# Two inner sums of the third head's products, issued directly behind the second head's last running sum

## The chip, the cores and the metric

The kernel runs on one core of a Trainium2 chip. The core has a matrix engine (TensorE, PE in the profile; its weight loads are listed as PEld), a vector engine (VectorE, DVE), an activation engine (ScalarE, ACT), GpSimd (POOL) and a sync engine (SP). Each works through a queue of its own in order. The metric is the device time of one execution in microseconds (us); several executions are timed and their median is taken. A profile is one execution recorded instruction by instruction.

## The reference

Sixteen images x of 512 channels by 32 x 32 positions (1024 positions) in float32:

```
xn  = group_norm(x, 8 groups)
q, k, v = qkv_w @ xn + qkv_b            # 1536 x 512 by 512 x 1024, per image
attn = softmax(q^T k / sqrt(128))       # 4 heads of 128 channels, 1024 x 1024 each
out = proj_w @ (attn v) + proj_b        # 512 x 512 by 512 x 1024
return x + out
```

## The kernel before, in words

**The loop.** The main loop runs over steps: 16 images, 4 heads of each (numbered 0 to 3), 8 key blocks j of each head. In a step, for each half of the 1024 queries, `scores` (L798) multiplies a block of k by q into PSUM, ACT takes the exponential (L804), and DVE adds the block of exponentials to a running sum `tot` (L810 for the first pair of blocks, L812 from j = 2 on). The instruction of each L812 is kept in `added[image, head, j]`. `weighted_sum` (L894) multiplies the exponentials of the step before by v into the PSUM tile `po`; behind a head's last block ACT copies `po` out (L901). A head that is over gets its denominators from `tot` (a transpose on L821, a reduction on L823, small operations from L826 to L835) and a division (L904).

**The products between.** All other matrix products are cut into units that are spread over the steps by `plan_head`. Head 0 of an image carries the q and k products of its own heads 2 and 3, head 1 the output projection of the image before, head 2 the q and k products for heads 0 and 1 of the next image, and head 3 the v product of the next image. So behind head 1's last step the projection of one image ends, and the q/k product of another begins.

**How such a product is computed.** `two_levels` uses Strassen's scheme in Winograd's form twice: seven outer products in four groups (`OUTER`: products 1 and 5, 2 and 6, 7 and 4, 3), and for each group seven inner products in the order 1, 2, 6, 5, 7, 4, 3 (`ORDER`). An inner product is two matrix products here, one for each outer product of the group, and each shows up as two PE instructions of 128 x 256 (L567). Inner products 1, 6, 7 and 4 gather in one PSUM bank (`x` in the profile's names, as `qk_x`), 2 alone and then 5 and 3 in another (`qk_y`). Between, ACT copies the `x` bank away (L461, `qk_p`, `qk_u`), and DVE adds the `y` bank to such a copy (L587, `qk_r`). Each inner product multiplies a weight factor by a block or by a sum of blocks (`FACTORS`): products 1, 2 and 3 use the blocks b11, b21 and b22 as they are, and

```
t1 = b12 - b11   (for product 5)       t2 = b22 - t1   (for product 6)
t3 = t2 - b11    (for product 7)       t4 = b21 - t2   (for product 4)
```

`make_sum` (L529 to L541) takes one such inner sum of a group: a `tensor_sub` on DVE of 128 x 256 for each of the group's outer products (L537), and where `sums == "keep"` a copy of it to DRAM, issued on POOL's queue (L541), which the v product reads later. `sums` is "keep" for the q/k products of heads 0 and 1 of every image but image 0, and these are the products that head 2 carries. For their group 0 (outer products 1 and 5) the first outer product reads the image's own tiles x, and the second reads an outer sum that lies in x too (L283 `x<-x`). Their first unit holds the group's weights, the sums t1 and t2 and inner product 1; the second unit t3 and product 2; the third t4 and product 6; the fourth product 5; the fifth product 7.

**The projection's end.** `finish` in `proj_groups` (L775) adds to each quarter of the result its bias and residual (L778) and a last part (L781), and sends it out with a DMA on POOL's queue (L782).

**What sets the order.** A scheduler lays down each engine's queue before the run. It goes by priority, which is the order of the program, among the instructions that its own model of time takes for ready; `tc.high_priority(URGENT)` moves what stands in its block 40 places forward in this priority, and `tc.issue_after(ins)` puts what stands in its block behind `ins` in the queue of that engine, which is an order and not a wait for a result. On the chip each queue is then worked off in that order.

Of the kernel before, what the change touches and what calls it, by code (L numbers as in the profile page):

```python
# [27 lines left out]
URGENT = 40  # L28
# [135 lines left out]
def fast_path(ctx, tc, x, sources, out, consts, flag, dims):  # L164
# [6 lines left out]
    nc = tc.nc  # L171
    B, C, N, NCC, NH2, NB, GC, SCALE = dims
# [324 lines left out]
    def two_levels(name, site, b, blocks, finish, sums="make", homes="BBBB", prepare=None):  # L497
# [13 lines left out]
        def sum_tile(g, m):  # L511
            k = int(m[1]) - 1
            tag = f"in_{m}" if homes[g] == "B" else f"ot{2 + k // 2}{k % 2}"
            if homes[g] == "C":
                if k % 2 == 0:
                    pairs[g] = ppool.tile([P, N], F32, tag="p", name=f"{name}_{g}_{m}")
                t = pairs[g][:, ts(k % 2, HALF)]
            else:
                t = tpool.tile([P, HALF], F32, tag=tag, name=f"{name}_{g}_{m}")
            haves[g][m] = t.rearrange("p (i q) -> p i q", q=Q)  # L520
            return haves[g][m][:, : len(OUTER[g])]

        def inner_block(g, i, m):
            if m[0] == "t":
                return haves[g][m][:, i, :]
            outer = blocks()[FACTORS[OUTER[g][i]][1]]
            return outer[int(m[1]) - 1][:, ts(int(m[2]) - 1, Q)]

        def make_sum(g, m):  # L529
            n = len(OUTER[g])  # L530
            to = sum_tile(g, m)
            a, c = {
                "t1": ("b12", "b11"), "t2": ("b22", "t1"), "t3": ("t2", "b11"),
                "t4": ("b21", "t2"),
            }[m]
            for i in range(n):
                nc.vector.tensor_sub(to[:, i, :], inner_block(g, i, a), inner_block(g, i, c))  # L537
            if sums == "keep":
                t = dpool.tile([P, n, Q], F32, tag=f"{m}_{g}", bufs=1, name=f"kept_{m}_{g}")
                inner_kept[b, g, m] = t  # L540
                nc.gpsimd.dma_start(t, to)  # L541

        def group_units(g):
# [12 lines left out]
            def inner_sum(m):  # L556
                if sums != "load" and m not in have:
                    make_sum(g, m)
# [57 lines left out]
        def first_sums(groups=(0,)):  # L616
            for g in groups:
                for m in ("t1", "t2", "t3", "t4"):
                    if sums == "load":
                        nc.sync.dma_start(sum_tile(g, m), inner_kept[b, g, m])  # L620
                    else:
                        make_sum(g, m)
# [165 lines left out]
    inverse, rows_of, added, exps = {}, {}, {}, {}  # L788
    steps = B * HEADS * NB

    def where(s):
        bh, j = divmod(s, NB)
        return (*divmod(bh, HEADS), j)
# [336 lines left out]
    for s in range(steps + 1):  # L1130
        units = []
        if s < steps:
            b, h, j = where(s)
# [9 lines left out]
        for half in range(NH2):  # L1143
# [11 lines left out]
            n = (len(units) + 1) // 2  # L1155
# [137 lines left out]
```

## Time and profile before

| what | value |
|---|---|
| median of 5 runs | 3181.52 us (3180.82 to 3183.71) |
| the profiled execution | 3181.88 us; span of its instructions 3180.0 us |
| PE busy | 3163.4 us, 99% of the span |
| DVE busy | 2630.4 us, 83% |
| ACT busy | 1440.6 us, 45% |
| POOL busy | 514.8 us, 16% |
| TensorE clock granted | 0.998 of full |

A line of the timeline gives start and length in us, engine, line of the kernel, operation, what it writes and reads, its shape, how many instructions of the kind were merged (x2), and in brackets how long the engine was idle before it and what ended that. Matrix products overlap each other, and the end of one is a model; the distance from one start to the next says how long the engine was taken.

### The profile page before, as it was taken

The page shows a single profiled execution, that of the slowest core. Times are in us where ns is not written, and L with a number is a line of the kernel's source. Part 1 is how long each engine was busy: PE and PEld are TensorE (multiplying, and loading weights), DVE is VectorE, ACT ScalarE, POOL GpSimd, SP SyncE. Part 2 cuts the span into 40 slices and gives each one's busy share as a digit, 9 for nine tenths or more (in the row PEclk, how much of TensorE's full clock was granted, in tenths as well). Part 3 has the DMA queues.
Part 4 walks back from the last instruction along what each step waited for, and adds up shares of the span by engine and source line. Part 5 has one row for each costly group of instructions (what it writes and reads, how often), then busy time and mean ns, then how long its engine had stood idle before and what let it go on. Part 6 is the DMA issues. An engine that isn't in the chain of part 4 may idle for free.

```text
span 3180.0 us, 34082 instructions
## 1 busy us (share of the span) xinstructions
PE 3163.4 (99%) x10496; PEld 2187.1 (69%) x10496; DVE 2630.4 (83%) x4634; ACT 1440.6 (45%) x2709; POOL 514.8 (16%) x893
## 2 busy tenths in 40 slices
PE   9999999999999999999999999999999999999999
PEld 7566676676766766677666677667676676766764
DVE  8878979788897888878888787987879978788784
ACT  2535435354353543535435454453534545344342
POOL 0011221111211112211122111222012221122200
PEclk9999999999999999999999999999999999999999
DMA  5655554545545555454554545555455564555631
GB/s 168 213 183 162 182 177 146 178 150 194 166 157 164 161 184 176 163 166 145 193 171 160 174 141 190 167 173 173 140 179 170 176 188 127 181 160 184 182 126 41
DMA packets 211308, 526.92 MB, mean 166 GB/s; under 512 B 32816, under 2 KB 65840, under 8 KB 211120
## 3 DMA queue, kind: packets, MB, share of 16 engines
q1 hardware_dynamic: 133312, 284.74, 29.5%
q0 software_dynamic: 63840, 204.53, 19.1%
q10 hardware_dynamic: 13968, 35.41, 3.5%
q8 instruction: 86, 1.41, 0.2%
q14 instruction: 102, 0.84, 0.1%
HBM read 389.56 MB, written 135.00 MB: 165 GB/s over the span
## 4 chain that ended last, share of the span: by engine, by line
PE 87%; DVE 10%; issue 2%; POOL 1%; DMA 1%; SPq 0%; ACT 0%; POOLq 0%; DVEq 0%
PE po L894 24%; PE s L798 24%; PE qk_x L567 12%; PE qk_y L567 9%; PE v_x L567 6%; PE v_y L567 4%; PE pp_x L567 4%; PE pp_y L567 3%; DVE y L781 2%; DVE tot L812 2%; DVE y L778 2%; DVE pp_r L587 1%; DVE pp_r L634 1%; POOL rstd L68 1%; DVE o L904 1%
## 5 line engine op out<-in xcount | busy, mean ns | idle before, releaser
L894 PE MATMUL po<-p,v 128*128 128x512 f32 x2048 | 1048.9, 594 | 0.0
L798 PE MATMUL s<-qk,qk 128*128 128x512 f32 x2048 | 1047.1, 593 | 1.3 <-ACT p L804 1.3
L804 ACT ACTIVATE p<-s 128x512 f32<-128x512 f32 x1024 | 610.3, 596 | 933.6 <-PE s L798 930.2
L894 PEld LDWEIGHTS po<-p,v 128*128 128x128 f32 x2048 | 602.9, 303 | 316.8 <-issue 212.2
L812 DVE TENSOR_TENSOR tot<-tot,p 128x1024 f32<-128x1024 f32 x385 | 469.2, 1219 | 161.6 <-ACT p L804 161.6
L798 PEld LDWEIGHTS s<-qk,qk 128*128 128x128 f32 x2048 | 387.6, 190 | 89.2 <-issue 28.0
L567 PEld LDWEIGHTS qk_x<-qk_t,w 128*128 128x128 f32 x1344 | 250.5, 190 | 171.5 <-issue 76.6
L567 PE MATMUL qk_x<-qk_t,w 128*128 128x256 f32 x1344 | 357.4, 382 | 1.1 <-ACT qk_u L461 1.1
L461 ACT COPY qk_u<-qk_x 128x512 f32<-128x512 f32 (+1 forms) x256 | 136.2, 532 | 230.6 <-PE qk_x L567 226.2
L731 POOL DMA_DIRECT2D vd<-vu x120 | 66.7, 557 | 908.6 <-DVE vu L723 901.3
L587 DVE TENSOR_TENSOR qk_r<-qk_y,qk_u 128x512 f32<-128x512 f32 (+1 forms) x256 | 157.8, 616 | 36.4 <-ACT qk_u L461 22.0
L567 PE MATMUL pp_x<-pp_t,w_proj 128*128 128x256 f32 x630 | 169.3, 385 | 0.0
L736 POOL DMA_DIRECT2D v<-vd x240 | 140.5, 592 | 170.4 <-DMA vd<-vu 74.9
L782 POOL DMA_DIRECT2D out_y<-y x120 | 66.0, 550 | 628.6 <-DVE y L781 626.5
L587 DVE TENSOR_TENSOR v_r<-v_y,v_u 128x512 f32<-128x512 f32 (+1 forms) x120 | 76.2, 635 | 110.6 <-ACT v_u L461 80.3
L567 PE MATMUL v_x<-v_t,w_v 128*128 128x256 f32 x630 | 166.6, 381 | 0.0
L541 POOL DMA_DIRECT2D kept_t<-qk_t x240 | 129.2, 540 | 223.5 <-DVE qk_t L537 204.0
L567 PEld LDWEIGHTS pp_x<-pp_t,w_proj 128*128 128x128 f32 x630 | 116.1, 190 | 64.1 <-issue 22.2
L567 PEld LDWEIGHTS v_x<-v_t,w_v 128*128 128x128 f32 x630 | 118.4, 190 | 55.3 <-issue 19.1
L567 PE MATMUL qk_y<-x,w 128*128 128x256 f32 x512 | 141.8, 379 | 0.0
L666 DVE SCALAR_TENSOR_TENSOR qk<-qk_r,qkb_sb,qk_r 128x512 f32<-128x512 f32 x192 | 137.6, 743 | 1.6
L461 ACT COPY v_u<-v_x 128x512 f32<-128x512 f32 (+1 forms) x124 | 66.2, 534 | 157.0 <-PE v_x L567 130.4
(204 smaller groups left out, 4481.3 us busy)
## 6 DMA issues: line engine op xcount, KB each, us to landing
kept_t<-qk_t POOLq DMA_DIRECT2D x180, 256.0 KB, 3.2
w<-kept SPq DMA_DIRECT2D x90, 512.0 KB, 4.2
v_t<-kept_t SPq DMA_DIRECT2D x180, 256.0 KB, 2.9
w<-kept SPq DMA_DIRECT2D x90, 384.0 KB, 3.5
rinv<-row ACTq DMA_DIRECT2D x63, 512.0 KB, 4.7
x<-in_x POOLq DMA_DIRECT2D x60, 512.0 KB, 5.0
vd<-vu POOLq DMA_DIRECT2D x120, 256.0 KB, 3.1
v<-vd POOLq DMA_DIRECT2D x240, 128.0 KB, 4.2
```

Of the source, the lines that this page charges most:

```text
L461: nc.scalar.copy(t[n][:, :width], t["x"][:, :width])
L541: nc.gpsimd.dma_start(t, to)
L567: nc.tensor.matmul(acc[:, ts(i, Q)], have["w"][t][:, i, slot, :], inner(i, bn), start=(first and i == 0), stop=True, skip_group_check=True,)
L587: nc.vector.tensor_add(dst, view(a), view(c))
L666: nc.vector.scalar_tensor_tensor(st[b, h][:, ts(half, HALF)], a, qkb_sb[:, i : i + 1], c, ALU.add, ALU.add)
L731: nc.gpsimd.dma_start(rows[which][ts(h, P), :], u)
L736: nc.gpsimd.dma_start(vs[b, pair][ts(q, BLK), half].rearrange("m h (k i) j -> m (h k) (i j)", k=n), rows[which].rearrange("(k m) (q e) -> ...
L782: nc.gpsimd.dma_start(out[b, ts(o, P), ts(half, HALF)], t)
L798: nc.tensor.matmul(sc, ks[b, h][:, ts(j, P)], qs[b, h][:, ts(half, HALF)], start=True, stop=True)
L804: exps[s] = nc.scalar.activation(ps[s][:, ts(half, HALF)], sc, AF.Exp, scale=SCALE)
L812: added[b, h, j] = nc.vector.tensor_add(tot[b, h][:, i], tot[b, h][:, i], ps[s][:, i])
L894: nc.tensor.matmul(po[b, h][:, i], v_block(b, h, j), ps[s][:, i], start=(j == 0), stop=(j == NB - 1),)
```

## The change

In `make_sum`, the subtractions of t1 and t2 of group 0 in the "keep" products stand now in two blocks: they are issued behind the last running sum of head 1 (`added[b - 1, 1, NB - 1]`; b is the image that the product belongs to, so b - 1 is the image whose heads are being worked off), and at a priority 40 places further forward. The arithmetic, the DMAs and all other instructions are as before.

```diff
-            for i in range(n):
-                nc.vector.tensor_sub(to[:, i, :], inner_block(g, i, a), inner_block(g, i, c))
+            with ExitStack() as order:
+                if sums == "keep" and g == 0 and m in ("t1", "t2"):
+
+
+                    order.enter_context(tc.issue_after(added[b - 1, 1, NB - 1].ins))
+                    order.enter_context(tc.high_priority(URGENT))
+                for i in range(n):
+                    nc.vector.tensor_sub(
+                        to[:, i, :], inner_block(g, i, a), inner_block(g, i, c)
+                    )
```

## The prediction

> **What bounds the kernel now.** First the page: its busy times, and the chain of work that ended last.
>
> ```profile
> PE 3163.4 (99%) x10496; PEld 2187.1 (69%) x10496; DVE 2630.4 (83%) x4634; ACT 1440.6 (45%) x2709; POOL 514.8 (16%) x893
> ...
> PE 87%; DVE 10%; issue 2%; POOL 1%; DMA 1%; SPq 0%; ACT 0%; POOLq 0%; DVEq 0%
> ```
>
> PE sets the time, and 10% of the chain runs through DVE: PE can gain only where it waits. So I read the chain itself in order of time, around the place the change touches: the start of the third head (head 2), here the fourth of fourteen such places. A line gives start, length, work.
>
> ```profile
> 932.46 1.13 DVE tot L812
> 933.60 0.60 DVE y L781
> 934.20 0.66 DVE y L778
> ...
> 935.80 0.35 DVE qk_t L537
> 936.15 0.04 issue
> 936.19 0.70 PE qk_y L567 x2
> ```
>
> From 910 us on, the chain lies on DVE. It comes back to PE at 936.19, through a subtraction on L537, the second half of t1. The timeline of PE and then of DVE shows the place whole:
>
> ```profile
> 934.58 1.02 PE L894 MATMUL po<-p,v 128*128 128x512 f32 x2
> 935.44 0.59 PE L567 MATMUL qk_y<-qk_t,w 128*128 128x256 f32 x2
> 936.19 0.70 PE L567 MATMUL qk_y<-qk_t,w 128*128 128x256 f32 x2 [0.16 <-DVE qk_t L537]
> 936.73 1.02 PE L798 MATMUL s<-qk,qk 128*128 128x512 f32 x2
> 937.58 1.03 PE L567 MATMUL qk_x<-qk_t,w 128*128 128x256 f32 x4
> 938.45 1.04 PE L894 MATMUL po<-p,v 128*128 128x512 f32 x2
> 939.32 1.10 PE L567 MATMUL qk_x<-qk_t,w 128*128 128x256 f32 x4
> 940.25 0.59 PE L567 MATMUL qk_x<-x,w 128*128 128x256 f32 x2
> ```
>
> ```profile
> 932.39 1.21 DVE L812 TENSOR_TENSOR tot<-tot,p 128x1024 f32<-128x1024 f32 x1
> 933.52 0.68 DVE L781 TENSOR_TENSOR y<-y,pp_r 128x512 f32<-128x512 f32 x1
> 934.12 0.74 DVE L778 SCALAR_TENSOR_TENSOR y<-pp_r,projb_sb,y 128x512 f32<-128x512 f32 x1
> 934.78 0.41 DVE L537 TENSOR_TENSOR qk_t<-x 128x256 f32<-128x256 f32 x1
> 935.12 0.68 DVE L781 TENSOR_TENSOR y<-y,pp_r 128x512 f32<-128x512 f32 x1
> 935.72 0.41 DVE L537 TENSOR_TENSOR qk_t<-x 128x256 f32<-128x256 f32 x1
> 936.06 0.68 DVE L587 TENSOR_TENSOR qk_r<-qk_y,qk_p 128x512 f32<-128x512 f32 x1
> 936.66 0.74 DVE L537 TENSOR_TENSOR qk_t<-x,qk_t 128x256 f32<-128x256 f32 x2
> 937.33 0.75 DVE L537 TENSOR_TENSOR qk_t<-qk_t,x 128x256 f32<-128x256 f32 x2
> ```
>
> DVE is never idle here (8.00 us busy between 930 and 938). Behind the last running sum (932.39) come two of the projection's last additions, the first half of t1 (934.78), an addition, the second half of t1 (935.72), the eviction L587, t2, t3. On PE, 935.44 is inner product 5, which needs t1: its second half starts 0.06 us behind the end of 935.72. Product 6 (937.58) needs t2; product 7 (939.32) needs t3 and ACT's copy of what 6 left in the bank.
>
> **What that wait costs.** The bracket says 0.16 us, measured from a modelled end; starts are better. Scores take 0.85 us (936.73 to 937.58), four instructions of 128 x 256 take 0.87 (937.58 to 938.45). From 935.44 to 937.58 PE does 0.87 + 0.85 = 1.72 us of work in 2.14: **0.42 us are lost**, 0.32 ahead of 936.19 and 0.10 inside that pair. A second loss follows: product 7 takes 0.93 us (939.32 to 940.25) for 0.87 of work, having waited for the copy of 6 (its weight load at 939.28 is put down to ACT qk_u), so 0.06.
>
> The place recurs in the timeline once an image, 196.2 us apart, behind each projection: in images 1 to 14, that is 14 times (image 0 has no projection before, image 15 no next image), as the waits on L537 count (PE qk_y, 14 times). Twelve lose 0.42. Two, at 739 and 2309 us, lose 0.56: 739.04 to 741.28 is 2.24 against 1.72, with 0.04 more ahead of it. Sum: 12 x 0.42 + 2 x 0.56 = **6.2 us**; with product 7's, 14 x 0.06 = 0.8, it is **7.0 us**.
>
> A rule of the Trainium skill makes the first figure smaller: TensorE: Matmul & The Clock Gate (section "Step-by-step: what each phase is for") says that PE pulls weight loads ahead of matmuls in flight. The weights for 936.19 would then have lain ready, and the wait would cost 0.32 us, together 14 x 0.32 = 4.5 us. The trace disagrees here: the weight load itself starts at 936.19, put down to DVE qk_t (0.56 us idle).
>
> **The change, part by part.** It removes and adds no instruction. *Moved:* four subtractions per place. By starts one takes 0.34 us (935.72 to 936.06; the two of t2, 936.66 to 937.33, take 0.67). Directly behind the last sum, DVE is at 933.52, so t1 lies ready near 934.3 and t2 near 934.9 (933.52 + 3 x 0.34 + 0.41). Their inputs are there: the outer sum in x (L283) starts last at 931.45. The buffers they write have held sums of the projection's operand; the last product that reads such a tile starts at 919.26.
>
> *On PE:* behind 934.58 both t1 and t2 are ready, so nothing is left to wait for at 935.44. I expect the laid-down order to change too: product 6 stands ahead of 5 in the program, and only a late t2 can have let 5 pass. At image 0, where no projection stands in front, PE does take the `qk_x` product first:
>
> ```profile
> 157.43 1.03 PE L567 MATMUL qk_y<-x,w 128*128 128x256 f32 x4
> 158.29 1.10 PE L567 MATMUL qk_x<-qk_t,w 128*128 128x256 f32 x4
> 159.24 1.03 PE L567 MATMUL qk_y<-qk_t,w 128*128 128x256 f32 x4
> ```
>
> Then 6 runs at 935.44, ACT has 2 us more for its copy, and product 7 loses its 0.06 no longer. If 5 still goes first, that 0.06 stays.
>
> *What becomes later:* two L781 and an L778 by 1.34 us (4 x 0.34), and L587 by up to 1.34, to about 937.4. For the additions only the DMAs to `out` on POOL wait, and the end of the kernel is far. L587 frees a `qk_y` bank; the next product to take it is one of group 1, at 945.41: 7 us to spare. That cover gone, every us would count in full. *POOL's queue:* the copies of t1 and t2 (L541, 0.54 us each) may pass two `out_y` issues; POOL is 16% busy, and the copies are read a head later. *SP's and ACT's queues* are passed by nothing. *The new order edge* is no wait: the subtractions stand on DVE behind a sum that was ahead of them before.
>
> *What is late next:* t3 for product 7. DVE's total is unchanged, so t3 ends near 938.1 or earlier, and 7 is due 0.43 + 0.06 us earlier than now, at 938.8: 0.7 us to spare. After that come t4 (939.20, for a product at 942.83) and sums with over 1 us.
>
> **The sum.** 3181.88 - 7.0 = 3174.9 us in the profiled execution. The median of the runs lies 0.36 us under that execution, so **3174.5 us** by the median. What the trace cannot show is the order that the scheduler lays down afterwards. Bounds from rows: below, one more of the small losses of an image goes, as that ahead of a projection product at 923.56 (0.13 + 0.10 us, 14 times 3 us: 3171.5); above, the gain is eaten by the next wait (nothing, 3181.5), or overtaken as in rival 4. I take the rows of the place itself.
>
> **The rivals.**
> 1. *Only the wait goes* (5 stays first): 3181.52 - 6.2 = 3175.3. For it: 5 is where it is now. Against it: image 0.
> 2. *The next wait takes part.* Product 7 finds t3 late, or a later bank is freed late, for about half the gain: 3178. For it: no wait of DVE is listed from 921.5 to 958.3 us, so it is behind through all of this stretch, and PE now comes sooner. Against it: 0.7 us of slack at t3, and no wait of PE for DVE between 937 and 958.
> 3. *The change does not do what it says*: the scheduler cannot place the four there, for instance because it holds the buffers taken. Then 3181.5. Against it: 919.26.
> 4. *Slower: t3 is overtaken.* Only t1 and t2 are moved forward. If, with the projection's additions pushed behind them, t3 is laid down behind the pair L283 (1.20 us, 938.00 to 939.20) and the transpose L821 (1.16, to 941.03), it ends near 940.4, and product 7, due at 938.8, stands 1.6 us, with 0.1 us of restart, PE's whole queue behind it: 14 x (1.7 - 0.5) = 17 us more, 3198. It decides from a t3 that ends later than 939.3, where the new wait equals the old. For it: DVE's queue is full here and the order is laid down by a model of time. Against it: t3 stands ahead of both in the program.
>
> **How the numbers follow.** About 0.2%, 6.4 us, is what a measurement of this kernel can tell from no change; the bound of faster is 3175.2, close to the forecast. Chances: the forecast 0.47 (its own range 3173.3 to 3176), rival 1 0.13, rival 2 0.22, rival 3 0.06, rival 4 0.12. Faster: four fifths of the forecast and half of rival 1, 0.44. Same: the rest of these, and rivals 2 and 3, 0.44. Slower: rival 4, 0.12. The range reaches from the lower bound, 3171.5, past no change with 1 us for the spread of the runs, to 3182.5; it leaves out rival 4 and little more.
>
> **What would show it.** In the new profile: four L537 in a row behind the L812 that is followed by L781; no wait of PE `qk_y` for DVE qk_t at the fourteen places; `qk_x<-qk_t` ahead of `qk_y<-qk_t` there; images 195.7 us apart instead of 196.2. I am wrong if a PE wait appears ahead of product 7 or in the 25 us behind it, or if other places of the image have changed their order.

## The result and the profile after

The changed kernel takes 3174.87 us (median of 22 runs, 3173.75 to 3176.08), the kernel before 3181.52 (42 runs beside them, 3180.13 to 3184.07): a ratio of 0.9978, 95% interval 0.9972 to 0.9984. The profiled execution of the changed kernel took 3174.49 us, its span is 3172.6 us, the granted clock 0.999. One of the twelve runs of `dose_t3` below took 10320.73 us at a granted clock of 0.338 and is left out of its ratio. Eight lines were added, so lines behind 541 have other numbers: the inner sums stand on L543, the products on L575, scores on L806, P.V on L902, the last running sum on L820, the last additions on L789 and L786, the eviction of the `y` bank on L595, ACT's copy of the `x` bank still on L461.

The page of the changed kernel, its busy times and the shares of the chain that ended last:

```profile
PE 3157.5 (100%) x10496; PEld 2191.2 (69%) x10496; DVE 2630.9 (83%) x4634; ACT 1441.6 (45%) x2709; POOL 516.5 (16%) x893
...
PE 98%; DMA 1%; DVE 1%; issue 0%; SPq 0%; ACT 0%; ACTq 0%; DVEq 0%
```

DVE's busy time is what it was, but its share of the chain went from 10% to 1%. The place itself, first PE's timeline and then DVE's (this execution is 1.58 us earlier here than the one of before):

```profile
933.00 1.02 PE L902 MATMUL po<-p,v 128*128 128x512 f32 x2
933.86 1.03 PE L575 MATMUL qk_x<-qk_t,w 128*128 128x256 f32 x4
934.73 1.03 PE L575 MATMUL qk_y<-qk_t,w 128*128 128x256 f32 x4
935.59 1.02 PE L806 MATMUL s<-qk,qk 128*128 128x512 f32 x2
...
937.30 1.03 PE L575 MATMUL qk_x<-qk_t,w 128*128 128x256 f32 x4
```

```profile
930.81 1.21 DVE L820 TENSOR_TENSOR tot<-tot,p 128x1024 f32<-128x1024 f32 x1
931.94 0.75 DVE L543 TENSOR_TENSOR qk_t<-x 128x256 f32<-128x256 f32 x2
932.61 0.75 DVE L543 TENSOR_TENSOR qk_t<-x,qk_t 128x256 f32<-128x256 f32 x2
...
935.49 0.42 DVE L543 TENSOR_TENSOR qk_t<-qk_t,x 128x256 f32<-128x256 f32 x1
935.82 0.68 DVE L595 TENSOR_TENSOR qk_r<-qk_y,qk_p 128x512 f32<-128x512 f32 x1
```

Product 6 (933.86) now stands ahead of 5 (934.73); each runs in 0.87 us, one behind the other, and nothing is listed in brackets. PE's order differs from before at these fourteen places and nowhere else. t1 and t2 are ready 0.5 us before the first of them. t3 has taken t1's old places between the additions: its second half (935.49) is ready 1.4 us ahead of product 7 (937.30).

**Where the time went.** I took the distance from each PE instruction's start to the next and subtracted what such a pair takes undisturbed (0.215 us for 128 x 256, 0.429 for 128 x 512). Over these two shapes, what is left over 0.03 us adds up to 29.6 us before and 22.9 after. At twelve of the fourteen places 0.32 + 0.105 us of product 5 are gone, at the other two 0.56, and at all fourteen 0.07 of product 7, 7.2 us together; images are 195.76 us apart instead of 196.27. Against that stands one larger loss: the first q/k product of image 0 waits 1.36 us for its weights from DRAM instead of 0.54, but it starts at 156.54 us as against 156.49. PE was 0.76 us earlier there, from before any changed instruction, and the transfer took that back. In the lists of waits of the kernels below, this one is anything from 0.4 to 1.3 us; I don't put it down to the change.

### The profile page after: what moved, and what is told of

Its sections match the earlier page's. It is cut to its first block, busy times and chain, and to the rows that moved or that the text cites. A ratio compares the mean times of both kernels' runs of the same rounds, so it can differ in the third digit from the quotient of the medians.

```text
span 3172.6 us, 34083 instructions
## 1 busy us (share of the span) xinstructions
PE 3157.5 (100%) x10496; PEld 2191.2 (69%) x10496; DVE 2630.9 (83%) x4634; ACT 1441.6 (45%) x2709; POOL 516.5 (16%) x893
## 3 DMA queue, kind: packets, MB, share of 16 engines
q1 hardware_dynamic: 133312, 284.74, 29.6%
## 4 chain that ended last, share of the span: by engine, by line
PE 98%; DMA 1%; DVE 1%; issue 0%; SPq 0%; ACT 0%; ACTq 0%; DVEq 0%
PE po L902 27%; PE s L806 27%; PE qk_x L575 12%; PE qk_y L575 9%; PE pp_x L575 6%; PE v_x L575 6%; PE v_y L575 4%; PE pp_y L575 4%; PE v_x L692 1%; PE lx L986 0%; PE v_y L692 0%; PE ly L986 0%; DMA w<-kept 0%; DMA kept_proj<-w_proj 0%; DMA wv_a<-in_qkv_wT 0%
## 5 line engine op out<-in xcount | busy, mean ns | idle before, releaser
L902 PE MATMUL po<-p,v 128*128 128x512 f32 x2048 | 1048.7, 594 | 0.0
L806 PE MATMUL s<-qk,qk 128*128 128x512 f32 x2048 | 1047.1, 593 | 1.3 <-ACT p L812 1.3
L902 PEld LDWEIGHTS po<-p,v 128*128 128x128 f32 x2048 | 603.9, 302 | 321.6 <-issue 215.5
L820 DVE TENSOR_TENSOR tot<-tot,p 128x1024 f32<-128x1024 f32 x385 | 469.8, 1220 | 161.2 <-ACT p L812 161.2
L806 PEld LDWEIGHTS s<-qk,qk 128*128 128x128 f32 x2048 | 387.6, 190 | 89.2 <-issue 28.0
L575 PEld LDWEIGHTS qk_x<-qk_t,w 128*128 128x128 f32 x1344 | 251.7, 190 | 167.7 <-issue 76.8
L575 PE MATMUL qk_x<-qk_t,w 128*128 128x256 f32 x1344 | 356.4, 382 | 1.1 <-ACT qk_u L461 1.1
L461 ACT COPY qk_u<-qk_x 128x512 f32<-128x512 f32 (+1 forms) x256 | 136.3, 533 | 229.1 <-PE qk_x L575 227.1
L595 DVE TENSOR_TENSOR qk_r<-qk_y,qk_u 128x512 f32<-128x512 f32 (+1 forms) x256 | 157.8, 617 | 36.4 <-ACT qk_u L461 21.9
L575 PE MATMUL pp_x<-pp_t,w_proj 128*128 128x256 f32 x630 | 169.3, 385 | 0.0
L595 DVE TENSOR_TENSOR v_r<-v_y,v_u 128x512 f32<-128x512 f32 (+1 forms) x120 | 77.0, 641 | 110.5 <-ACT v_u L461 80.3
L575 PE MATMUL v_x<-v_t,w_v 128*128 128x256 f32 x630 | 166.6, 381 | 0.0
L575 PEld LDWEIGHTS pp_x<-pp_t,w_proj 128*128 128x128 f32 x630 | 116.1, 190 | 64.2 <-issue 22.2
L575 PEld LDWEIGHTS v_x<-v_t,w_v 128*128 128x128 f32 x630 | 118.4, 190 | 55.3 <-issue 19.1
L575 PE MATMUL qk_y<-x,w 128*128 128x256 f32 x512 | 141.8, 379 | 0.0
L731 DVE STREAM_TRANSPOSE vu<-vt 128x512 f32<-128x512 f32 x120 | 135.6, 1130 | 2.6 <-DMA vd<-vu 2.5
```

The costliest lines, as they stand in the source:

```text
L461: nc.scalar.copy(t[n][:, :width], t["x"][:, :width])
L575: nc.tensor.matmul(acc[:, ts(i, Q)], have["w"][t][:, i, slot, :], inner(i, bn), start=(first and i == 0), stop=True, skip_group_check=True,)
L595: nc.vector.tensor_add(dst, view(a), view(c))
L731: nc.vector.transpose(u.rearrange("p (q i j) -> p j q i", q=n, i=BLK), t.rearrange("p (j q i) -> p j q i", q=n, i=BLK),)
L806: nc.tensor.matmul(sc, ks[b, h][:, ts(j, P)], qs[b, h][:, ts(half, HALF)], start=True, stop=True)
L820: added[b, h, j] = nc.vector.tensor_add(tot[b, h][:, i], tot[b, h][:, i], ps[s][:, i])
```

## How a late operand is paid for

PE's weight loads (PEld) show it. The kernel before, its load for the second half of product 5, and the changed kernel, its first load of product 6:

```profile
936.19 0.30 PEld L567 LDWEIGHTS qk_y<-qk_t,w 128*128 128x128 f32 x2 [0.56 <-DVE qk_t L537]
```

```profile
933.43 0.19 PEld L575 LDWEIGHTS qk_x<-qk_t,w 128*128 128x128 f32 x1
```

A load that waits for nothing starts with the matmul before it (933.43, its own matmul at 933.86). A load that waits starts when it is let go (936.19), its matmul is listed at the same time, and the next matmul follows 0.32 us later instead of 0.215. So the wait cost its 0.32 us and 0.105 more. What came late is not what this load reads: by the kernel it loads the weight factor `w` (128 x 128), while t1 is the operand that the product then streams (128 x 256). Yet the trace shows the wait for t1 on the load, so the load could not run ahead either. Whether the 0.105 us would go if only the matmul waited was not tried. In the trace of after a load that began 0.02 or 0.03 us ahead of its matmul of 128 x 256 (90 of them) cost 0.084 or 0.082 us on average, and one that began 0.21 ahead cost 0.001: lead and loss add up to about 0.106. This was the working rule of the later runs, for the inner products: **a product loses (when its load is let go) + 0.106 - (when it is due), if that is above 0**. Part of it is not listed as a wait at all, because the load began before the product was due.

## The experiments

All are compared with the kernel before on their own chip; its medians there were 3181.58 to 3181.64 us.

| kernel | median us | ratio to before, 95% interval |
|---|---|---|
| after | 3174.87 | 0.9978 (0.9972 to 0.9984) |
| e_six | 3178.15 | 0.9988 (0.9979 to 0.9998) |
| e_five | 3174.67 | 0.9978 (0.9969 to 0.9987) |
| e_t1 | 3183.32 | 1.0005 (0.9996 to 1.0014) |
| drop_adds | 3183.75 | 1.0006 (0.9997 to 1.0015) |
| prio_only | 3178.05 | 0.9989 (0.9980 to 0.9998) |
| dose_t3_1 | 3174.57 | 0.9977 (0.9968 to 0.9986) |
| dose_t3 | 3177.54 | 0.9987 (0.9978 to 0.9995) |
| dose_t3_3 | 3184.64 | 1.0008 (0.9999 to 1.0017) |
| e_late | 3173.35 | 0.9973 (0.9963 to 0.9984) |
| n5 | 3171.80 | 0.9968 (0.9956 to 0.9980) |
| late_n5 | 3169.45 | 0.9963 (0.9950 to 0.9976) |

The intervals reach 2 to 4 us to each side. A smaller difference between two kernels is read from their traces; the medians only agree with it.

**e_six: only PE's order.** Against the kernel before; `make_sum` is left as it was. In the function that issues a product (`have["six"]` is the last instruction of product 6):

```diff
+                    if j == 5 and sums == "keep" and g == 0 and b > 1:
+                        order.enter_context(tc.issue_after(have["six"].ins))
```

> The kernel before, with one edit: at the fourteen places inner product 5 is pinned behind inner product 6 on PE, so that PE goes scores, P.V, 6, 5 there. No sum is moved on DVE: t1 and t2 stand between the projection's last additions as before. Theory A (what was lost was PE's own queue standing behind a product whose operand came late; it is enough that the late operand is met later): 6 is reached near 937.15 us of the fourth place and t2's halves are ready near 937.1 and 937.4, so the 0.42 us a place go and at most product 7's 0.06 stays: 3174.9 to 3176, no wait of PE for t1 or t2 left. Theory B (the sums themselves must be made earlier): no gain, 3181.5. Theory C (the gain comes from the additions being pushed back, or from the out transfers behind them, which do not move here): no gain, 3181.5.

It took 3178.15 us: half of the gain, and no theory had that. PE's listed wait for t1 and t2 is gone, as A said. But scores and P.V now follow each other without a product between them, and two other loads come late. PE and then PEld of this kernel:

```profile
935.48 1.23 PE L907 MATMUL po<-p,v 128*128 128x512 f32 x2
```

```profile
935.45 0.54 PEld L907 LDWEIGHTS po<-p,v 128*128 128x128 f32 x2 [0.65 <-ACT o L914]
936.30 0.87 PEld L578 LDWEIGHTS qk_x<-qk_t,w 128*128 128x128 f32 x4 [0.30 <-DVE qk_t L543]
...
938.24 0.73 PEld L578 LDWEIGHTS qk_x<-qk_t,w 128*128 128x128 f32 x4 [0.21 <-ACT qk_u L461]
```

P.V's load waits for ACT's copy of the finished head out of `po`, and the next start is 0.21 us late; product 7's load waits for the copy of 6, 0.08 us. 14 x 0.29 = 4.0 us; the kernel is 3.3 us above after. Products 5 and 6 had covered that copy. Nor did t2 come in good time: product 6's load was let go only at 936.30, and without P.V's 0.21 us the product would have been due at 936.33, so by the rule about 0.08 us would have been lost there. So it isn't enough to let PE meet a late operand later: what stood in between was itself the cover for something else. B and C, which gave no gain without a move on DVE, are wrong too.

**e_five: the order of 5 and 6 turned back.**

```diff
+            p6, p5 = (p5, p6) if sums == "keep" and g == 0 and b > 1 else (p6, p5)
```

> The kernel after, with one edit: at the fourteen places product 5 stands ahead of product 6 again, as it did before; t1 and t2 stay directly behind the last running sum. Theory A (the wait for t1 is the gain; the order of 5 and 6 is only worth product 7's wait for ACT's copy of 6, 0.06 us): 14 x 0.06 = 0.8 us given back, 3175.7. Theory B (the order of the products is what brought it, as PE would come to the late sum later): most of the gain is gone, above 3179. If product 7's wait was never real: 3174.9.

3174.67 us, nothing given back. PE laid down 5, 6, scores, P.V, 7, so that 7 had 1.7 us behind 6 and its wait didn't return. What cost product 7 its 0.07 us was that only one P.V lay between 6 and 7; the order of 5 and 6 by itself is worth nothing that shows here.

**e_t1: only t1 moved.**

```diff
-                if sums == "keep" and g == 0 and m in ("t1", "t2"):
+                if sums == "keep" and g == 0 and m in ("t1",):
```

> The kernel after, with only t1 moved; t2 stays where it was in the program, behind the additions. PE then lays down half of 6, half of 5, the other half of 6, the other half of 5. Theory A (PE stands wherever the first operand it meets comes late): t2 takes t1's place as what is waited for; its first half is ready near 937.1 while PE is there near 936.3 or earlier: 0.5 us and more a place lost again, no gain, 3181.5 to 3183.5, and the wait is listed against the subtraction of t2. Theory B (t1 alone carried the wait of before, t2 has slack): 3175 to 3177.

3183.32 us, as A. PE of this kernel:

```profile
935.51 0.67 PE L575 MATMUL qk_x<-qk_t,w 128*128 128x256 f32 x2 [0.41 <-DVE qk_t L543]
```

By starts 0.57 us are lost ahead of it (0.72 at two of the fourteen places) and 0.08 inside: 9.4 us, where the median lies 8.5 above after. The wait moved on to t2, which PE now met first.

**drop_adds: less work on DVE, sums not moved.** Against the kernel before:

```diff
-            nc.vector.tensor_add(t, t, c)
+            if which != "c12": nc.vector.tensor_add(t, t, c)
```

> The kernel before, without the last addition of one quarter of the projection's result (the top right one, images 0 to 14, two instructions of 128 x 512 an image; that quarter lacks this term). DVE has 1.2 us less to do just ahead of the sums, and lays them as: one of the final additions, t1's first half, an eviction, t1's second half, t2. PE lays 6 ahead of 5 and both together, as in after. Theory A (what counts is only when the operand that PE meets first is ready): t2's first half is ready near 935.9 in the times of the fourth place, its product stands ready at 935.44: 0.49 and 0.1 us lost, 0.6 a place instead of 0.42 and 0.06: 3182 to 3183.5, no faster than before though there is less work. Rival (the amount of DVE work ahead of the sums is what the change takes out of the way): t1 and t2 earlier, 3175 to 3177.

3183.75 us with 1.2 us less for DVE at each place: as A, 0.25 above its range. PE of this kernel, which leaves one term out of a quarter of the result:

```profile
936.75 1.10 PE L575 MATMUL qk_x<-qk_t,w 128*128 128x256 f32 x4 [0.41 <-DVE qk_t L543]
```

It is not the amount of work ahead of the sums that counts. Less of it let PE's order change to 6 first, t2 was then late for 6, and 0.57 us were lost ahead of it and 0.08 inside.

**prio_only: the order edge left out.**

```diff
-                    order.enter_context(tc.issue_after(added[b - 1, 1, NB - 1].ins))
```

> The kernel after without the order edge: t1 and t2 are only given a high priority. DVE then takes t1 ahead of the last running sum, between x's outer sum, and t2 behind it; the running sum comes about 0.34 to 0.67 us later, and two products near it change places on PE. Theory A (only the operands that PE meets matter): product 5 and 6 find t1 and t2 ready, no gain is lost, 3174.9. Rival (the edge is needed: sums taken ahead of the running sum hold it up, and with it what waits for it or for the outer sums): 3176 to 3179, with a new wait of PE just ahead of the place.

3178.05 us: the rival's number and its new wait, but not its cause. On DVE the first half of t1 goes as far ahead as 922.32, where the projection's last sum `pp_t` stood, and `pp_t` comes at 928.74 instead of 922.08. So PE lays a `pp_y` product ahead of the one that needs `pp_t`, and its bank isn't free yet. PEld of this kernel:

```profile
928.27 0.30 PEld L575 LDWEIGHTS pp_y<-o,w_proj 128*128 128x128 f32 x2 [0.76 <-DVE pp_r L595]
```

By starts 0.21 + 0.105 us a place are lost, 14 x 0.315 = 4.4 us. Nothing on PE waited for the running sum. What the edge does is to keep the urgent sums from passing the projection. The edge without the priority was not run, so what it does alone isn't shown.

**dose_t3_1, dose_t3, dose_t3_3: t3 later by steps.** The second half of t3's subtraction is done k times more at the fourteen places (k = 1, 2, 3).

```diff
-                for i in range(n):
+                for i in (*range(n - 1), *[n - 1] * (k + 1 if sums == "keep" and g == 0 and b > 1 and m == "t3" else 1)):
```

> The kernel after, with the second half of t3's subtraction done three times instead of once at the fourteen places: 0.67 us more work for DVE at each, 9.4 us in all, PE's order unchanged. Theory A (DVE has slack everywhere but where an operand is met late; t3 is ready over 1 us before product 7): 3174.9, within 1 us, and no new wait. Rival (DVE is behind in this stretch, so its work counts, as the next wait): up to 14 x 0.67 = 9.4 us more, 3184.

3177.54 us: 2.7 above after, between the two theories. t3 wasn't ready in time: the repeats had been laid behind an eviction and half of an outer sum, which A had overlooked. DVE and PEld of this kernel:

```profile
938.61 0.42 DVE L543 TENSOR_TENSOR qk_t<-qk_t,x 128x256 f32<-128x256 f32 x1
```

```profile
939.08 0.30 PEld L575 LDWEIGHTS qk_x<-qk_t,w 128*128 128x128 f32 x2 [0.33 <-DVE qk_t L543]
```

The second half of product 7 was due at 938.99 (0.43 behind 938.56) and its load was let go at 939.08: 0.09 + 0.105 = 0.19 us, 14 x 0.19 = 2.7 us. That is the whole difference, so the 9.4 us of added work cost nothing by themselves. Or does added work count at a rate? Two more doses tell these apart:

> The kernel after, with the second half of t3's subtraction done twice instead of once at the fourteen places: 0.335 us more for DVE at each, 4.7 us in all, PE's order unchanged. It goes behind the eviction, so t3 is ready near 938.1 in the times of the kernel with two repeats, where its load has to begin at 938.88. Theory A, with the rule that a product loses (time at which its load is let go) + 0.106 us - (time at which it is due), where that is over 0: nothing is lost, 3174.9, within 0.7 us. Rival (DVE's added work counts by itself, with 2.67 us for 9.4 us of it measured): 1.3 us more, 3176.2.

> The kernel after, with the second half of t3's subtraction done four times instead of once: 1.0 us more for DVE at each place, 14 us in all. The last repeat stands behind both halves of the outer sum L283, so t3 is ready near 940.03 in the times of the kernel with two repeats; PE takes a product of x between the halves of product 7, so the second half is due at 939.42. Theory A, by the same rule: 940.03 + 0.106 - 939.42 = 0.72 us a place, 14 x 0.72 = 10.0 us over after: 3184.9. Rival (added DVE work counts in proportion, 2.67 us for 9.4): 4.0 us, 3178.9.

3174.57 and 3184.64 us: A both times. With k = 1 there are 4.7 us more work and no more time; the theories are closer together there than the interval, but the trace shows product 7 with nothing lost (0.87 us, from 938.75 to 939.62). With k = 3 PE and DVE show:

```profile
940.50 0.70 PE L575 MATMUL qk_x<-qk_t,w 128*128 128x256 f32 x2 [0.43 <-DVE qk_t L543]
```

```profile
940.03 0.42 DVE L543 TENSOR_TENSOR qk_t<-qk_t,x 128x256 f32<-128x256 f32 x1
```

By starts 0.60 + 0.105 = 0.70 us a place, where 0.72 had been worked out. DVE's time is free here up to the point where a sum reaches PE too late, and from there the sum's lateness counts in full.

**e_late, late_n5, n5: the same rule at other places.** In the trace of after, product 6 of the projection's third group waits for ACT's copy (0.13 + 0.105 us an image), and two q/k products an image lose 0.085 us with no wait of PE listed. PE and PEld of after at one of these:

```profile
964.85 1.11 PE L575 MATMUL qk_x<-qk_t,w 128*128 128x256 f32 x4
965.79 1.03 PE L902 MATMUL po<-p,v 128*128 128x512 f32 x2
```

```profile
964.83 0.73 PEld L575 LDWEIGHTS qk_x<-qk_t,w 128*128 128x128 f32 x4 [0.65 <-ACT qk_u L461]
```

`e_late` moves the projection's product 6 one P.V product later, `n5` the q/k products, and `late_n5` both:

```diff
+                if b > 0:                                    # e_late, late_n5 (head 1)
+                    plan[6].insert(5, plan[6].pop(2))
-            n = (len(units) + 1) // 2                        # n5, late_n5
-            run(units[half * n : (half + 1) * n])
+            n = (len(units) + 1) // 2 - (s > NB and s < steps and j == 5 and h != 3)
+            run(units[half * n : n if half == 0 else None])
```

> The kernel after, with one more edit elsewhere: the unit with product 6 of the projection's third group, which waits each image for ACT's copy (0.13 us ahead and 0.105 behind, 14 times in the trace of after), is moved behind the next weighted sum, one PV product later. Theory A (such a short wait of PE costs its whole length plus about 0.1 us, and goes whole when other ready work is put in front): 14 x 0.235 = 3.3 us less than after, 3171.6. Rival (the wait goes to the product put in front or to the next one, as ACT's later copy is late for product 7): same as after, 3174.9.

3173.35 us, 1.5 below after: half of what A gave. PEld of this kernel:

```profile
926.62 0.30 PEld L575 LDWEIGHTS pp_x<-pp_t,w_proj 128*128 128x128 f32 x2 [0.54 <-ACT pp_u L461]
```

The copy of 6 is later too, and product 7's load begins only 0.01 us ahead of its matmul: 0.10 us come back, 14 x (0.235 - 0.10) = 1.9 us. The rival named this product and had too large a price for it.

> The kernel with product 6 of the projection's third group one weighted sum later, with one more edit: in the sixth step of heads 0 to 2 one unit less is laid in front of the second weighted sum. On PE this swaps one product with the P.V product behind it, at two places an image (near 964.9 and 1062.5 us in the trace of after), 31 in all; the order on DVE and ACT stays what it was. At those places the trace of after shows no wait listed, but 0.085 us lost between the first and the second instruction. Theory A (the weight load of the first instruction was let go too late by ACT's copy; a load has to begin about 0.106 us ahead of its matmul to cost nothing, and what is missing of that is added): with a P.V product of 0.86 us in front all 0.085 go, 30 x 0.085 = 2.55 us: 3170.8. Rival (the 0.085 is a property of that pair of instructions, not of a late load): 3173.3, and the same 0.085 at the product's new place.

> The kernel after, with only the edit to the sixth step of heads 0 to 2: one unit less in front of the second weighted sum, which swaps one product with the P.V product behind it at 31 places; product 6 of the projection's third group stays where it was. Theory A: 30 x 0.085 us, 2.55 us less than after: 3172.3. Rival (the gain measured with both edits came from the other one, or needs it): 3174.9.

3169.45 and 3171.80 us. In the trace of n5 the loss of the 30 products is gone, for the one at 964.85 too, which now stands at 965.02 behind a P.V product. So it was no property of the pair:

```profile
964.17 1.02 PE L902 MATMUL po<-p,v 128*128 128x512 f32 x2
965.02 1.03 PE L575 MATMUL qk_x<-qk_t,w 128*128 128x256 f32 x4
965.89 1.03 PE L575 MATMUL qk_y<-xt,w 128*128 128x256 f32 x4
```

n5 is 3.1 us below after for 2.55 worked out; late_n5 is 3.9 below e_late, and 5.4 below after, where the two edits alone sum to 4.6. The runs of one kernel spread by 1 to 3 us, so I don't read these remainders. late_n5 has the lowest median of all kernels here.

## Why the prediction was right, point by point

- **The time.** 3174.5 forecast, 3174.87 measured; in the profiled execution 3174.9 against 3174.49. That both agree to 0.4 us is partly luck: 7.2 us are gone at the fourteen places, and image 0's wait for its weights, which the sum left out, differs by up to 0.9 us from trace to trace.
- **What the wait costs.** Twelve times 0.42, twice 0.56 and fourteen times 0.07 us: an image is 0.51 us shorter, where 0.50 had been worked out. The wait inside (0.10) is as real as the one ahead of it, as dose_t3 and dose_t3_3 show. The rule from the Trainium skill, TensorE: Matmul & The Clock Gate (section "Step-by-step: what each phase is for"), holds here for a load that waits for nothing (933.43) and not for one that carries its product's wait (936.19); by it product 5's part of the gain would have been 4.5 us (an estimate, 14 x 0.32), where 6.2 are gone.
- **The moved work.** By the distance from the P.V product ahead of the place (934.58 before, 933.00 after), the first L789 and L595 come 1.34 us later, exactly the four subtractions, and no wait of PE for them is listed.
- **The new order on PE** came as forecast, 6 ahead of 5. It wasn't needed: in e_five 5 comes first. Rival 1's premise, and the prediction's own, that product 7 keeps its 0.06 us in that case, was wrong; what counts is what lies between 6 and 7.
- **t3's slack** was mis-sized on the safe side. I put it at 0.7 us, from the end of DVE's queue; t3 went into t1's gaps instead, its second half ready at 935.91 for a product due at 937.73. By the rule of 0.106 that leaves about 1.7 us. Rivals 2 and 4 both hung on it. dose_t3 shows what 2 would have looked like: it had to push t3 back by 1.9 us for 0.19 us of wait.
- **Rival 3** is refuted by the four L543 behind L820.
- **The chain from 910 to 936 us** was read a little too simply: 1.9 us of it, at 918.5, lie on GpSimd (`rstd`, L68). The place itself is not touched by that.

Not settled: why a P.V load that came late in e_six cost 0.21 us with 0.02 us of lead, twice what the loads of the inner products cost. The traces point at how v lies in memory. In image 0, where `v_block` reads v without gaps, three P.V loads with the same lead are listed with 0.19 us and cost 0.085; in the later images, where it reads every fourth element, the loads are listed with 0.31 us and cost 0.207. No kernel with another layout of v was run.

## What to carry to other kernels

On a full engine, look at what it meets first, not at how much work the other engine has. A late operand costs its lateness and the part of its product's weight load that no longer hides, and starts tell that better than listed waits do. Before a product is moved, ask what it was covering: in e_six the products taken out of the gap had hidden a copy, and half of the gain went there.

## What the runs showed of the hardware that was not expected

The exposed part of an inner product's late weight load is 0.105 us, though the trace lists that load with 0.186 us, and it shrinks one for one with the lead (0.026 us of lead, 0.080 lost; 0.009 of lead, 0.097 lost). The Trainium skill, TensorE: Matmul & The Clock Gate (section "LDWEIGHTS (loading the stationary operand)"), gives a load of P columns P / 1.2 ns, an estimate of 0.107 us for 128 columns; the rows here agree with that, and not with the listed length.
